# A fused four-layer kernel: in layer 0, x in one tile per half of the channels, convolutions in even steps, the result's projection in two parts, layer norms one chunk ahead

## The chip, the cores and the metric

The kernel runs on one core of a Trainium2 chip. The metric is the device time of one execution in microseconds (us), as the median over executions. The engines are named as in the profile: PE (TensorE), with its weight loads PEld, DVE (VectorE), ACT (ScalarE), POOL (GpSimd) and SP (SyncE), which here issues nearly all DMA transfers. Each engine works through its own queue in program order; semaphores order one engine against another.

## The reference, cut to what matters

Four layers follow each other on a tensor x of 2 x 128 x 64 x 64 (batch, channels, height, width), all in float32. The change touches layer 0 alone: a layer norm over the channels, four selective scans (Mamba) with the same weights over the 4096 positions of each image, row by row and column by column, each forward and reversed, and a fused projection that is added to x.

```python
xz = x @ W_in.T
xh, z = jnp.split(xz, 2, axis=-1)                 # 256 channels each
xc = causal_depthwise_conv(xh, conv_w) + conv_b   # 4 taps
xh = silu(xc)
x_dbl = xh @ W_xp.T                               # dt (8), B (16), C (16)
dt = softplus(dt @ W_dt.T + b_dt)
dA = exp(dt[..., None] * A)                       # 256 channels x 16 states
dBu = dt[..., None] * Bm[:, :, None, :] * xh[..., None]
h = dA_t * h + dBu_t                              # the scan over positions
y = einsum('lbdn,bln->bld', hs, Cm) + xh * Dp
y = y * silu(z)
return y @ W_out.T                                # then W_fuse, b_fuse, + x
```

Layer 1 and layer 2 are attention over 4096 positions, layer 3 is a small Mamba over channel groups with a group norm.

## The kernel before, in words

Layer 0 cuts the positions into chunks of T = 512. There are 2 images x 2 orders (by rows, by columns) x 2 directions x 8 = 64 chunks, one after the other; the list `chunks` (L432) has eight forward chunks, then eight reversed ones, and so on. The channels (256) lie in two halves `i` of 128 partitions. For the scan, channels and states are regrouped into 16 units `u` of 128 partitions x 1024 elements, and one unit is done in each of the 16 steps `s` of a chunk.

The order of all work is written out by hand (`manual_schedule`, L447). In step `s` of chunk `c` the loop emits, on each engine's queue:

- POOL: `s_dbu(s+2)` (L336), the product of `dus` and `bs` into one of three `dbu` buffers; `s_hc(s-1)` for the units 1, 5, 9, 11 and 14 (L390).
- DVE: `s_scan(s)` (L380), then what the table `V` holds for this step, then `s_hc(s-1)` for the other units (L392). After step 2 the old chunk's second half is gated with `yg_(1)`, after step 10 this chunk's first half with `yg_(0)` (L410).
- ACT: `s_da(s+1)` (two exponentials, L349), `s_fix(s+1)` (L361, L364), `s_hst(s-1)` (L385), then what the table `A` holds.
- PE: `s_pc` in odd steps (L369), `y0` (L396), `s_y` for pairs of units (L403; the pairs 4,5 in step 8 and 6,7 in step 9), then what the table `M` holds.
- SP: the spreads of dt and dt*x (`dts`, `dus`) and of the rows of B and C (`bs`, `cs`) for the next chunk.

The tables hold the work on three other chunks: the rest of the chunk before (`old`), the step sizes of the next chunk (`new`: `pt`, `abs_`, `dt_`, `dtu_`, and `pz`, `z_` for forward chunks), and the convolution of the chunk after it (`nxt`). The convolution is four matmuls per half with the taps folded into the weights, `px(i)` (L238); ACT moves the result with its bias into SBUF, `x_(i)` (L244); later come one `xsilu` over both halves (L257) and the projection `pd` (L273).

Each PSUM bank is in use: four for `da`, two for `pc`, one for `y`, one for `misc`. So all of `px`, `pz`, `pt`, `pd`, `po` and the layer norm's matmuls share one `misc` buffer, and each has to wait until the one before it has been read. The tile `xs` (both halves, 128 x 2 x 512) has two buffers, so `x_` of chunk k+2 writes where the `xs` of chunk k was, whose last readers are `y0(0)` in step 3 and `y0(1)` in step 11.

`y0` adds the skip term with a diagonal matrix, `s_y` sums the states into `y`, `yg_` multiplies with the gate, `po` (L412) projects both halves and adds x through the identity, all into `misc`, and `xo` (L426) writes x back. The layer norm of a chunk (`Norm0`: `center`, `sub`, `square`, `var`, `keep`, `ln`, `exp`, `rows`, `scale`, `mul`, `affine`) is spread over the end of one chunk and the beginning of the next; the first three are done ahead of the loop. Norms are in flight in chunks 0 to 5 and 15 to 23 (counted from 0).

```python
                if nxt is not None:
                    M[9], A[10] = lambda: nxt.px(0), (lambda: nxt.x_(0),)
                    M[11], A[12] = lambda: nxt.px(1), (lambda: nxt.x_(1),)
                    A[13] = (nxt.xsilu,)
                    M[15] = nxt.pd
```

Of the kernel before, what the change touches and what calls it, by code (L numbers as in the profile page):

```python
# [13 lines left out]
P = 128  # L14
B, C, H, W = 2, 128, 64, 64
L = H * W
T = 512
# [5 lines left out]
ND = 73  # L23
# [33 lines left out]
def conv_seq_kernel(ctx: ExitStack, tc: tile.TileContext, a: dict, out: bass.AP):  # L57
# [36 lines left out]
    with ExitStack() as c0:  # L94
# [9 lines left out]
        def wt(tag, bufs=None, shape=(P, 2, T)):  # L104
            return wk_.tile(list(shape), F32, tag=tag, name=tag, bufs=bufs)
# [110 lines left out]
        class Chunk:  # L216
# [4 lines left out]
            def __init__(self, b, order, rev, q):  # L221
                self.b, self.order, self.rev = b, order, rev
                self.first, self.last = q == 0, q == NCH - 1
                self.ci = NCH - 1 - q if rev else q
                self.t0 = self.ci * T
                self.src = xnt if order else xn

                self.beg, self.sec = (T - 1, 0) if rev else (0, 1)
                self.dbu, self.h, self.hc = {}, {}, {}
                self.bs, self.cs, self.dts, self.dus = {}, {}, {}, {}  # L230
                self.pt_, self.y, self.pc = {}, {}, {}


            def px(self, i):
# [4 lines left out]
                       start=(k == 0), stop=(k == 3))  # L239

            def x_(self, i):
                if i == 0:
                    self.xs = wt("xs")
                act(self.xs[:, i, :], self.px_, AF.Identity, bias=v(f"cb{i}"))  # L244

            def pz(self, i):
                self.pz_ = misc()
# [6 lines left out]
                nc.scalar.copy(self.sz[:, i, :], self.pz_)  # L254

            def xsilu(self):
                act(self.xs, self.xs, AF.Silu)  # L257

            def zsilu(self):

# [8 lines left out]
            def pd(self):  # L269

                self.p = misc()
                for i in range(2):
                    mm(self.p[:ND], lhsT=w_xpT[:, i, :], rhs=self.xs[:, i, :],  # L273
                       start=(i == 0), stop=(i == 1))

            def xd_(self):
# [39 lines left out]
            def dtu_(self, i):  # L316
                if i == 0:
                    self.dtu = wt("dtu", 1)
                    self.ddu = dr.tile([2, P, T], F32, tag="ddu", name="ddu")
                nc.gpsimd.tensor_mul(self.dtu[:, i, :], self.dt[:, i, :], self.xs[:, i, :])  # L320
                nc.sync.dma_start(self.ddu[i], self.dtu[:, i, :])

            def spread(self, what, i):
# [69 lines left out]

            def y0(self, i):
                self.y[i] = ps.tile([P, T], F32, tag="y", name="y")
                mm(self.y[i], lhsT=diag_d[:, i, :], rhs=self.xs[:, i, :], start=True,  # L396
                   stop=False, skip_group_check=True)

            def s_y(self, u):
# [9 lines left out]
                    self.yg = wt("dt", 1)  # L409
                nc.vector.tensor_mul(self.yg[:, i, :], self.sz[:, i, :], self.y[i])  # L410

            def po(self):  # L412
                d = 2 * self.order + self.rev
                p = self.pp = misc()
                for i in range(2):
                    mm(p, lhsT=wof[:, i, d, :], rhs=self.yg[:, i, :], start=(i == 0), stop=False)
                if self.order:
                    xo = x[:, self.b, :].rearrange("p (h w) -> p w h", w=W)
                    xo = xo[:, self.ci * 8 : self.ci * 8 + 8, :]
                    p = p.rearrange("p (w h) -> p w h", h=H)  # L420
                else:
                    xo = x[:, self.b, self.t0 : self.t0 + T]
                mm(p, lhsT=ident, rhs=xo, start=False, stop=True)
                self.xo_ = xo, p

            def xo(self):  # L426
                if self.order == 0 and not self.rev:
# [6 lines left out]
        nk = len(chunks)  # L434
        norms, gates = {}, {}
        for j in range(NCH):
            if j > 2:
                norms[j - 3] = Norm0(0, j)
            norms[15 + j] = Norm0(1, j)
        turns = {k: k % 8 for k in (*range(6, 14), *range(32, 40))}  # L440

# [3 lines left out]
            pairs.setdefault(max(m + (3 if m in POOL_HC else 2) for m in (u, u + 1)), []).append(u)  # L445

        with tc.manual_schedule():  # L447
            for j in range(3):
                n = Norm0(0, j)
                for f in (n.center, n.sub, n.square, n.var, n.keep, n.ln, n.exp, n.rows, n.scale,  # L450
                          n.mul, n.affine):
                    f()
            c, c1 = chunks[:2]
            for i in range(2):
                c.px(i)
# [27 lines left out]
            c.s_dbu(1)  # L483
            c.s_da(0)
            c.s_fix(0)
            for i in range(2):
                c1.px(i)
                c1.x_(i)
# [3 lines left out]
            for k, c in enumerate(chunks):  # L492
                new, nxt = (chunks[k + i] if k + i < nk else None for i in (1, 2))
                ln, lp = norms.get(k), norms.get(k - 1)

                def at(u):
                    return (c, u) if 0 <= u < 16 else ((old, u + 16) if u < 0 else (new, u - 16))

                A, V, M, G = {}, {}, {}, {}
                if old is not None:
                    M[3], A[4] = old.po, (old.xo,)
                if c.rev:
                    A[4] = (*A[4], c.zload)
                else:
                    A[8] = (c.zsilu,)
                if new is not None:
                    A[0] = (new.xd_,)
                    M[0], A[1] = lambda: new.pt(0), (lambda: new.abs_(0),)  # L510
                    M[1], A[2] = lambda: new.pt(1), (lambda: new.abs_(1), new.e_exp)
                    A[3] = (new.e_ln,)
                    M[4], V[5] = lambda: new.pt(0), lambda: new.dt_(0)
                    M[5], V[6] = lambda: new.pt(1), lambda: new.dt_(1)
                    G[7], G[8] = lambda: new.dtu_(0), lambda: new.dtu_(1)
                    if not new.rev:
                        M[6], A[7] = lambda: new.pz(0), (lambda: new.z_(0),)
                        M[13], A[14] = lambda: new.pz(1), (lambda: new.z_(1),)
                if nxt is not None:
                    M[9], A[10] = lambda: nxt.px(0), (lambda: nxt.x_(0),)  # L520
                    M[11], A[12] = lambda: nxt.px(1), (lambda: nxt.x_(1),)
                    A[13] = (nxt.xsilu,)
                    M[15] = nxt.pd
                if lp is not None:
                    A[3] = (*A[3], lp.ln, lp.exp)
                    A[6] = (lp.rows,)
                    M[7], V[8] = lp.scale, lp.mul
                    A[9] = (lp.affine,)
                if ln is not None:
                    M[12], V[13] = ln.center, ln.sub  # L530
                    A[14] = (*A.get(14, ()), ln.square)
                    M[14], A[15] = ln.var, (ln.keep,)
                if k in turns:
                    A[11] = (lambda: turn(turns[k]),)

                for s in range(16):
                    (c1, u1), (c2, u2), (cp, up) = at(s + 1), at(s + 2), at(s - 1)

                    if c2 is not None:
                        c2.s_dbu(u2)  # L540
                    c.s_scan(s)
                    if s in V:
                        V[s]()
                    if cp is not None:
                        cp.s_hc(up)
                    if s in G:
                        G[s]()

                    if c1 is not None:
                        c1.s_da(u1)  # L550
                        c1.s_fix(u1)
                    if cp is not None:
                        cp.s_hst(up)
                    for f in A.get(s, ()):
                        f()

                    if s % 2 and s < 15:
                        c.s_pc(s + 1)
                    elif s == 15 and new is not None:
                        new.s_pc(0)  # L560
                    if s in (3, 11):
                        c.y0(s // 11)
                    for cy, e in ((c, s), (old, s + 16)):
                        for u in pairs.get(e, ()) if cy is not None else ():
                            cy.s_y(u)
                            cy.s_y(u + 1)
                    if s in M:
                        M[s]()

                    if s == 2 and old is not None:  # L570
                        old.yg_(1)
                    if s == 10:
                        c.yg_(0)

                    if new is not None:
                        if s in (7, 14):
                            new.spread("dts", s // 14)
                        if s in (9, 13):
                            new.spread("dus", s // 13)
                        if s in (8, 10, 12, 14):  # L580
                            new.states(0, s // 2 - 4)
                        if s in (11, 12, 13, 15):
                            new.states(1, GROUPS_C[{11: 0, 12: 1, 13: 2, 15: 3}[s]])
                old = c
            c.s_hc(15)
            for e in (16, 17):
                for u in pairs.get(e, ()):
                    c.s_y(u)
                    c.s_y(u + 1)
            c.yg_(1)  # L590
            c.po()
            c.xo()

# [890 lines left out]
```

## Time and profile before

| what | value |
|---|---|
| time, median of 3 runs | 7136.85 us (7136.01 to 7143.56) |
| the profiled execution's own time | 7116.64 us |
| its span | 7114.9 us |
| PE busy over the span | 6064.8 us (85%) |
| DVE busy | 5525.5 us (78%) |
| POOL busy | 5366.2 us (75%) |
| ACT busy | 4446.3 us (62%) |
| layer 0's scans, first start to last | about 106 to 3795 us |

The span runs from the first to the last instruction; the execution's own time is 1.7 us more, and the median of the unprofiled runs is 20.2 us above the profiled execution. Busy shares are means over stages with different limits, so the stage of the change, layer 0, is read by itself and chunk by chunk. In the timeline a row is a group of equal instructions: its start, its length, engine, line, output and inputs, count, and in brackets the idle time of the engine ahead of it with what ended that. A float32 matmul is two records on PE, so a convolution half (four matmuls) is a row of x8.

### The profile page before, as it was taken

Reading aid. Unit: us, or ns where it says so; the run is one execution under the profiler, and the core shown is the slowest. Engines: PE = TensorE matmul, PEld = TensorE weight load, DVE = VectorE, ACT = ScalarE, POOL = GpSimd, SP = SyncE. Lnnn points to the kernel's source line nnn. Section 1 sums busy time; section 2 is a strip of 40 time slices with the busy share of each in tenths; the row PEclk is TensorE's granted clock in tenths of the full one; section 3 lists DMA queues with packets and bytes.
Section 4 is the critical chain, followed back from the end, with each engine's and each line's share of the span. In section 5 each row is a group of like instructions: output and inputs, shape, how many; then the busy total and the mean of one; then the engine's idle time right before and its main releaser. Section 6 shows DMA issues by size and latency. Waiting matters only on the chain. (4 is left out here: it accounts for less than half of the span.)

```text
span 7114.9 us, 67194 instructions
## 1 busy us (share of the span) xinstructions
PE 6064.8 (85%) x20656; PEld 2821.4 (40%) x20656; DVE 5525.5 (78%) x4494; ACT 4446.3 (62%) x7622; POOL 5366.2 (75%) x2487
## 2 busy tenths in 40 slices
PE   6877778887788877888777999999999998889898
PEld 2222222222222222222223887788778886222222
DVE  3889888888898898989895666566556665778787
ACT  4777777777777777787675565455456555443443
POOL 3889888888998889989995666555556665777676
PEclk7777777777777777777777999999999999898898
DMA  4555555555555555555552000000000000222222
GB/s 121 133 134 139 134 131 134 134 137 134 137 142 141 141 139 144 138 134 140 144 143 76 1 5 2 1 1 1 1 1 1 13 1 30 79 75 70 91 67 77
DMA packets 352651, 616.50 MB, mean 87 GB/s; under 512 B 72473, under 2 KB 74786, under 8 KB 351906
## 3 DMA queue, kind: packets, MB, share of 16 engines
q1 hardware_dynamic: 351552, 610.44, 32.8%
q8 instruction: 162, 2.65, 0.2%
q14 instruction: 199, 1.63, 0.1%
q10 hardware_dynamic: 738, 1.78, 0.1%
HBM read 496.45 MB, written 115.47 MB: 86 GB/s over the span
## 5 line engine op out<-in xcount | busy, mean ns | idle before, releaser
L336 POOL TENSOR_TENSOR dbu<-dus,bs 128x1024 f32<-128x1024 f32 x1024 | 2402.2, 2359 | 422.2 <-DVE h L380 357.7
L380 DVE TENSOR_TENSOR_SCAN h<-da,hst,dbu 128x1024 f32<-128x1024 f32 x896 | 2093.1, 2342 | 355.2 <-ACT dbu L364 218.4
L349 ACT ACTIVATE da<-dts,aneg 128x512 f32<-128x512 f32 (+1 forms) x2048 | 1409.3, 688 | 304.1 <-DVE h L380 266.0
L826 POOL TENSOR_TENSOR sum<-sum,sc 128x1024 f32<-128x1024 f32 x384 | 905.8, 2359 | 495.9 <-ACT sc L821 492.2
L788 ACT COPY sc<-s 128x512 f32<-128x512 f32 x1024 | 597.0, 584 | 867.6 <-PE s L783 755.0
L369 PE MATMUL pc<-xd,sel 16*128 16x512 f32 x1024 | 760.8, 831 | 360.4 <-DVE hc L392 357.8
L783 PE MATMUL s<-q,k 128*128 128x256 f32 x4096 | 1057.5, 382 | 11.7 <-ACT q L769 8.4
L838 PE MATMUL av<-sc,v 128*128 128x256 f32 x4096 | 1049.6, 379 | 2.2 <-ACT sc L821 2.2
L795 DVE TENSOR_TENSOR mx<-mx,s 128x512 f32<-128x512 f32 x896 | 609.2, 680 | 569.1 <-ACT sc L788 568.1
L392 DVE TENSOR_TENSOR hc<-h,pc 128x1024 f32<-128x1024 f32 x704 | 841.5, 1195 | 0.1
L783 PEld LDWEIGHTS s<-q,k 128*128 128x128 f32 x4096 | 780.7, 191 | 146.1 <-issue 36.6
L838 PEld LDWEIGHTS av<-sc,v 128*128 128x128 f32 x4096 | 769.1, 190 | 103.1 <-ACT sc L821 3.7
L403 PE MATMUL y<-hc,cst 128*32 128x512 f32 x4096 | 766.3, 785 | 5.3 <-POOL hc L390 3.1
L390 POOL TENSOR_TENSOR hc<-h,cs 128x1024 f32<-128x1024 f32 x320 | 754.9, 2359 | 1.3 <-issue 1.3
L1153 POOL TENSOR_TENSOR A<-A,D 128x1024 f32<-128x1024 f32 x224 | 525.6, 2363 | 224.9 <-DVE D L1158 200.2
L818 DVE TENSOR_TENSOR sc<-sc,pm 128x1024 f32<-128x1024 f32 x512 | 620.1, 1212 | 0.9 <-PE pm L814 0.9
L821 ACT ACTIVATE sc<-sc 128x1024 f32<-128x1024 f32 x512 | 542.0, 1059 | 8.6 <-DVE sc L818 8.1
L1146 ACT ACTIVATE A<-dtr,aneg 128x1024 f32<-128x1024 f32 (+1 forms) x256 | 245.8, 1031 | 379.1 <-PE y L1178 361.6
L369 PEld LDWEIGHTS pc<-xd,sel 16*128 16x128 f32 x1024 | 186.6, 226 | 704.9 <-issue 291.3
L293 PE MATMUL misc<-xd,w_dt 9*128 9x512 f32 x512 | 335.5, 739 | 131.8 <-ACT xd L278 49.5
L1130 PE MATMUL q<-xs,lb 32*128 32x512 f32 x896 | 330.5, 710 | 70.4 <-DVE D L1140 64.2
L1164 DVE TENSOR_TENSOR A<-A,q 128x1024 f32<-128x1024 f32 (+1 forms) x256 | 276.6, 1080 | 138.5 <-PE q L1130 138.3
(210 smaller groups left out, 8070.2 us busy)
## 6 DMA issues: line engine op xcount, KB each, us to landing
dts<-ddt SPq DMA_DIRECT2D x512, 256.0 KB, 4.8
dus<-ddu SPq DMA_DIRECT2D x512, 256.0 KB, 4.8
bs<-rows SPq DMA_DIRECT2D x1024, 64.0 KB, 4.8
cs<-rows SPq DMA_DIRECT2D x1024, 64.0 KB, 3.1
ddt<-dt SPq DMA_DIRECT2D x128, 256.0 KB, 2.0
ddu<-dtu SPq DMA_DIRECT2D x128, 256.0 KB, 2.3
dtr<-ddt SPq DMA_DIRECT2D x448, 64.0 KB, 1.9
rx<-ddx SPq DMA_DIRECT2D x448, 64.0 KB, 1.9
```

The source lines that it names most:

```text
L336: nc.gpsimd.tensor_mul(t, self.dus[q], _bc(self.bs[g], 1, [P, 2, T]))
L349: act(t[:, i, sl], self.dts[q][:, i, sl], AF.Exp, scale=an[:, g, 2 * q + i : 2 * q + i + 1])
L369: mm(t, lhsT=sel[32:48, 4 * g : 4 * g + 4, :].rearrange("p n d -> p (n d)"), rhs=self.xd[32:48, :], start=True, stop=True)
L380: nc.vector.tensor_tensor_scan(ho, ai, bi, init, ALU.mult, ALU.add)
L390: nc.gpsimd.tensor_mul(t, self.h[u], _bc(self.cs[gq(u)[0]], 1, [P, 2, T]))
L392: nc.vector.tensor_mul(t, self.h[u], _bc(self.pc[u // 2], 1, [P, 2, T]))
L403: mm(self.y[q // 2][r : r + 32, :], lhsT=sum4, rhs=self.hc[u][:, i, :], start=False, stop=(u % 8 >= 6), skip_group_check=True)
L783: mm(p[:, o, :], lhsT=j.k[m // 8][:, m % 8 * P : m % 8 * P + P], rhs=self.q, start=True, stop=True)
L795: nc.vector.tensor_max(self.mx, self.s[0][:, 0:2, :] if u == 1 else self.mx, self.p[u])
L818: nc.vector.tensor_sub(s, s, _bc(self.pm[:, :], 1, [P, 4, NQ]))
L826: nc.gpsimd.tensor_add(self.sum, self.s[0] if w == 1 else self.sum, self.s[w])
L838: mm(self.av, lhsT=self.job.v[m // 8][:, m % 8, :], rhs=self.s[u // 2][:, m % 4, :], start=(m == 0), stop=(m == 31))
```

## The change

- `xs` becomes two tiles, one per half, each with two buffers. `xsilu` becomes two instructions.
- `px(0)`, `px(1)` go from steps 9 and 11 to steps 8 and 10; `x_(0)` from step 10 to step 9, `x_(1)` stays in step 12. `affine` goes from step 9 to step 10.
- `po` is cut in two: `po_x` (x through the identity, now first) in step 2, the two projections in step 3. `y0(0)` goes from step 3 to step 4.
- Layer norms of the first image run one chunk earlier: the norm of chunk 3 is done ahead of the loop, after the first `s_da` and `s_fix`, and norms are in flight in chunks 0 to 4. Those of the second image stay.

```diff
@@ Chunk
             def x_(self, i):
-                if i == 0:
-                    self.xs = wt("xs")
-                act(self.xs[:, i, :], self.px_, AF.Identity, bias=v(f"cb{i}"))
+                self.xs[i] = wt(f"xs{i}", shape=(P, T))
+                act(self.xs[i], self.px_, AF.Identity, bias=v(f"cb{i}"))
...
             def xsilu(self):
-                act(self.xs, self.xs, AF.Silu)
+                for t in self.xs.values():
+                    act(t, t, AF.Silu)
...
-            def po(self):
-                d = 2 * self.order + self.rev
-                p = self.pp = misc()
-                for i in range(2):
-                    mm(p, lhsT=wof[:, i, d, :], rhs=self.yg[:, i, :], start=(i == 0), stop=False)
+            def po_x(self):
+                self.pp = p = misc()
...
-                mm(p, lhsT=ident, rhs=xo, start=False, stop=True)
+                mm(p, lhsT=ident, rhs=xo, start=True, stop=False, skip_group_check=True)
                 self.xo_ = xo, p
+
+            def po(self):
+                for i in range(2):
+                    mm(self.pp, lhsT=wof[:, i, 2 * self.order + self.rev, :], rhs=self.yg[:, i, :],
+                       start=False, stop=(i == 1), skip_group_check=True)
@@ norms
-            if j > 2:
-                norms[j - 3] = Norm0(0, j)
+            if j > 3:
+                norms[j - 4] = Norm0(0, j)
@@ ahead of the loop
             c.s_da(0)
             c.s_fix(0)
+            norm(3)
             for i in range(2):
                 c1.px(i)
                 c1.x_(i)
@@ in the loop
                 if old is not None:
-                    M[3], A[4] = old.po, (old.xo,)
+                    M[2], M[3], A[4] = old.po_x, old.po, (old.xo,)
...
                 if nxt is not None:
-                    M[9], A[10] = lambda: nxt.px(0), (lambda: nxt.x_(0),)
-                    M[11], A[12] = lambda: nxt.px(1), (lambda: nxt.x_(1),)
+                    M[8], A[9] = lambda: nxt.px(0), (lambda: nxt.x_(0),)
+                    M[10], A[12] = lambda: nxt.px(1), (lambda: nxt.x_(1),)
                     A[13] = (nxt.xsilu,)
                     M[15] = nxt.pd
                 if lp is not None:
                     A[3] = (*A[3], lp.ln, lp.exp)
                     A[6] = (lp.rows,)
                     M[7], V[8] = lp.scale, lp.mul
-                    A[9] = (lp.affine,)
+                    A[10] = (lp.affine,)
...
-                    if s in (3, 11):
+                    if s in (4, 11):
                         c.y0(s // 11)
```

The readers `pd`, `dtu_` and `y0` take `self.xs[i]` for `self.xs[:, i, :]`, and the last chunk calls `po_x` ahead of `po`.

## The prediction

> **What bounds the kernel now.** First I read the windows view over single chunks of layer 0: chunk 36 (forward, no norm), chunk 59 (reversed, no norm) and chunk 19 (with a norm).
>
> ```profile
> core 0: us, PE busy (x) PEld busy (x) DVE busy (x) ACT busy (x) POOL busy (x), PEclk, DMA share, GB/s
> 2214.90:2272.90 58.00, 47.29 (x123) 13.19 (x122) 51.26 (x32) 46.10 (x89) 51.26 (x24) 0.74 0.54 138
> 3521.70:3579.40 57.70, 45.26 (x125) 11.85 (x118) 51.04 (x33) 40.78 (x81) 51.27 (x24) 0.71 0.56 138
> 1226.30:1287.70 61.40, 50.82 (x135) 14.64 (x136) 52.50 (x34) 47.99 (x98) 51.49 (x24) 0.75 0.52 130
> ```
>
> A chunk takes 57 to 61 us, and no engine is busy for more than 52.5. DVE and POOL are the nearest bounds at 51; the other 6 us are stalls. So next the waits of DVE, ACT and POOL over layer 0 (us in total, times, longest).
>
> ```profile
> DVE h L380 <- ACT dbu L364: 218.4, 193, 4.6
> DVE h L380 <- ACT hst L385: 148.6, 38, 4.8
> ACT xs L244 <- PE y L396: 413.9, 62, 7.9
> POOL dbu L336 <- DVE h L380: 357.7, 310, 3.0
> ```
>
> The scan on DVE waits for ACT, and ACT's longest wait is `x_` for `y0`, 62 times: once in each chunk that has a `nxt`. POOL only waits for the scan. The timeline of chunk 59, steps 9 to 12, shows how the one becomes the other.
>
> ```profile
> 3553.29 2.04 PE L369 MATMUL pc<-xd,sel 16*128 16x512 f32 x2 [4.71 <-DVE hc L392]
> 3555.26 1.94 PE L403 MATMUL y<-hc,cst 128*32 128x512 f32 x8
> 3557.12 5.55 PE L238 MATMUL misc<-xnt,wk 128*128 128x512 f32 x8
> 3558.69 0.66 DVE L410 TENSOR_TENSOR dt<-sz,y 128x512 f32<-128x512 f32 x1
> 3562.60 1.12 PE L369 MATMUL pc<-xd,sel 16*128 16x512 f32 x2
> 3563.65 1.12 PE L396 MATMUL y<-xs,diag_d 128*128 128x512 f32 x2
> 3564.82 0.69 ACT L244 ACTIVATE xs<-misc,vec 128x512 f32<-128x512 f32 x1 [7.57 <-PE y L396]
> 3565.40 1.41 ACT L349 ACTIVATE da<-dts,aneg 128x511 f32<-128x511 f32 x2
> 3567.22 4.59 DVE L380 TENSOR_TENSOR_SCAN h<-da,hst,dbu 128x1024 f32<-128x1024 f32 x2 [4.49 <-ACT hst L385]
> ```
>
> `x_(0)` is ready for its data at 3562.7, when `px(0)` ends, but writes into the `xs` buffer that `y0(1)` still has to read, and PE does that one step later. `da(12)` stands behind it on ACT, so scan 12 starts 4.49 us late. Reading this idle ahead of scan 12 in every chunk gives 242 us in 62 chunks: 4.02 on average in the 30 reversed chunks without a norm, 3.92 in the 19 forward ones without, 3.61 in the 13 with one. The other idle ahead of scans is 63 us at step 5 (the tables for `e_ln`), 42 at step 15 (the tables for `xsilu`) and 32 at step 2 (`pd`), which the change leaves alone.
>
> **The change, part by part.**
>
> *xs in two tiles.* `y0(0)` reads its half in step 4 and `x_(0)` writes in step 9; `x_(1)` stays in step 12, behind `y0(1)` of step 11. The wait of 6 to 8 us on ACT goes. The bytes are the same. One more ACT instruction per chunk: 1.06 us becomes two of 0.59 to 0.69 (the 512-wide rows of lines 300, 175 and 244), +0.12 to +0.32 us on the path at step 15, 7 to 20 us in 62 chunks. Against it, `da(14)` followed `x_(1)` 0.31 us after scan 12 had ended (3569.88 against 3569.57) and need not any more. I take zero, and -12 to +19 for the range.
>
> *px one step earlier.* Now `x_(0)` waits for `px(0)` instead, with `da(11)`, `s_fix(11)` and so scan 11 behind it on ACT; and on PE `pc(10)` and the `s_y` of units 6 and 7 stand behind `px(0)`, with `yg_(0)` on DVE waiting for them. So I walk the queues. `px(0)` starts when `s_y` of units 4 and 5 ends (the `misc` buffer is free by then): 3548.58 in chunk 59, 2245.10 in chunk 36, 1261.81 in chunk 19. It takes 5.0 us (the mean of the rows 5.55, 5.54, 4.35 in these chunks and 4.72 in chunk 15), `pc(10)` and `s_y` 2.1 more (1.12 and 1.06 at full clock). So `y` is ready at 3555.7, 2252.2, 1268.9; `yg_(0)` ran at 3558.69, 2251.65, 1267.34. Late by nothing (3.0 us of cover), 0.6 and 1.6 us. `x_(0)` ends 0.7 after `px(0)`, `da(11)` and its fix take 1.8: 2252.6 in chunk 36 against scan 11 at 2252.23 before, inside the 0.6. `x_(1)`: `px(1)` (3.70) follows `s_y`, then `pc(12)` and `y0(1)` (1.12 each), all done about 6 us after `yg_(0)`; scan 14, the first behind it, comes about 8.5 later (scans 11 to 13, two `hc`). Free. If the cover is gone, each us that PE is late at step 9 costs a us in that chunk.
>
> *What is late next.* With scan 12 moved up by 4, POOL must hold: after scan 5 it ran without a gap to 3567.54 in chunk 59, then waited 2.11 and 0.94 us for DVE. Without the stall it goes on, and `dbu` 13, 14, 15 end at about 3562.9, 3565.2 and 3569.9, each before its scan (3565, 3568, 3572). DVE stays the bound. `dus` for the next chunk lands at 3563.6 and is first read at 3572.0: 8.4 us of slack, of which 2 to 4 go.
>
> *po in two, y0(0) later.* The matmuls are the same. `po_x` waits for `abs_(1)` to free `misc` (3531.3), about when PE took up `y0` before (3531.5); `pc(4)` behind it has until step 5. `xo` waited for PE only 15 us in total over the kernel. Zero; with the cover gone at most the 1.9 us of the identity matmuls per chunk, which would come back at the wait of ACT's tables at step 5.
>
> *Norms ahead.* Chunk 5 loses its norm: it took 59.6, those after it 56.9, so -2.5. Ahead of the loop, PE takes norm 3 before `px` of chunk 1. `square` can start when `da(0)` ends at 100.58; from `square` to the end of `mul` the first norm took 10.05 (22.33 to 32.38), so `px` starts at 110.6, not 95.88. ACT's `da(1)` and scan 1 stand behind: +14.8 us once (10 if it overlaps better).
>
> No moved step issues a DMA, so SP's queue keeps its order.
>
> **Sum.** 242 removed, less 19 x 0.6 = 11 and 13 x 1.6 = 21, plus 2.5, less 14.8: 198 us. Against the profiled execution's own 7116.64 that is 6919; the unprofiled median stands 20.2 above it, so I forecast 7136.85 - 198 = 6939. Its own range, with the two costs of `px` between zero and double and the bounds above, is 6895 to 6995.
>
> **Clock, row and rule.** PE's clock decides how long `px(0)` takes. In chunk 36 the windows view shows:
>
> ```profile
> 2239.90:2243.30 3.40, 3.40 (x8) 0.63 (x10) 3.40 (x3) 2.76 (x8) 3.40 (x3) 0.50 0.20 77
> 2246.70:2250.20 3.50, 3.50 (x11) 0.58 (x10) 3.34 (x3) 3.42 (x7) 3.50 (x2) 0.50 1.06 270
> 2250.20:2253.60 3.40, 3.40 (x5) 1.34 (x5) 3.40 (x3) 0.94 (x3) 3.40 (x3) 0.50 1.05 321
> 2253.60:2257.00 3.40, 3.40 (x9) 1.05 (x7) 2.08 (x2) 0.00 (x0) 3.40 (x2) 1.00 1.07 237
> ```
>
> PE is busy throughout a stretch (the number behind the comma), yet the granted clock (third from last) is half until `px(0)` has filled a stretch. The Trainium skill ("TensorE: Matmul & The Clock Gate", Part 1) says that one busy window of some 3.4 us lifts the gate; here `pc` and `s_y` on part of the array did not lift it, and where they differ I go by the rows.
>
> **Rivals.**
> - *A warm convolution.* PE has no pause ahead of `px(0)` any more and runs it at full clock, 3.70 as `px(1)` does. Late by 0, 0 and 0.3 us: 242 - 4 + 2.5 - 14.8 = 226, 6911. By the skill's rule the time would come out here. For it: chunk 19 turned fast while `s_y` and `px(0)` shared a stretch. Against it: the rows above. 0.18.
> - *Half the stall stays.* Of ACT's 7.57 us, only the 2.15 behind `px(0)` (3562.67 to 3564.82) are `y0` and `pc`; if ACT gets to `x_(0)` ahead of a late `px(0)` as it does now, 2 us per chunk are won: 124 + 2.5 - 14.8 = 112, 7025. Against it: PE stood idle 4.71 us before `pc(10)` in chunk 59. This is also the case in which the split tile does not do what it says. 0.12.
> - *A cold convolution.* `px(0)` at half clock is twice the row of four records (3.62 for `po`), 7.0 with the overlap taken off, then 2.07 and 1.94: `y` is late by 0.7, 4.2 and 5.3 us. 242 - 21 - 80 - 69 + 2.5 - 14.8 = 60, 7077. 0.09.
> - *Slower.* The cold case, and PE reaches step 8 late as well, since 47 us of PE work at this clock then fill 53 us instead of 58. Each us late costs 62; from 1 us on the kernel is slower, and at 2 us it is 60 - 124 = -64: 7201. Against it: what PE waits for ahead of step 8 (`dt_`, the `hc` of unit 5) is set by DVE and POOL. 0.05.
>
> **Numbers.** The forecast has 0.56. The range 6880 to 7045 takes in the warm and the half case and leaves 0.14 and some edges out. Differences of up to 0.2% (14 us) count as no change, about what a measurement of this kernel can tell. All cases but the last are faster by more; between the cold and the slower case lie a few in a hundred: faster 0.92, same 0.03, slower 0.05.
>
> **What would show it.** Right: line 244 no longer waits for line 396, no idle ahead of scan 12, at most 2 us ahead of scan 11 in norm chunks, reversed chunks of 53 us, scan 1 at about 127 instead of 112. Wrong: `yg_` or scan 11 waiting for PE by 2 us or more in most chunks, POOL waited for by the scan, or chunks still at 57.

## The result

| | before | changed |
|---|---|---|
| median of the runs shown together | 7139.19 us (7136.01 to 7143.56) | 6914.52 us (6907.13 to 6921.35) |
| ratio, 95% interval | | 0.9685 (0.9668 to 0.9701) |
| span of the profiled execution | 7114.9 us | 6919.6 us |
| layer 0, up to the end of the last write of x | 3803.45 us | 3592.20 us |
| the rest (layers 1 to 3, same code) | 3311.4 us | 3327.4 us |

The kernel is 225 us faster; 198 were forecast. In the profiles layer 0 alone lost 211 us, and the other layers, whose code is the same, took 16 us longer. Over all 14 profiles of this study those layers took between 3311 and 3333 us, so a profiled span is compared best up to the end of layer 0. Below, "layer 0's end" is that point; two executions of the changed kernel put it at 3592.20 and 3595.45.

The windows view of the changed kernel, over one chunk each: the forward chunk 36, the reversed chunk 59 and the norm chunk 19.

```profile
core 0: us, PE busy (x) PEld busy (x) DVE busy (x) ACT busy (x) POOL busy (x), PEclk, DMA share, GB/s
2093.60:2147.90 54.30, 46.29 (x126) 12.41 (x122) 51.18 (x32) 46.31 (x90) 51.22 (x24) 0.78 0.58 147
3324.50:3378.50 54.00, 45.59 (x125) 11.68 (x118) 51.11 (x33) 41.09 (x82) 51.73 (x24) 0.75 0.59 149
1163.30:1221.30 58.00, 49.44 (x135) 14.22 (x134) 52.58 (x34) 48.30 (x98) 51.44 (x24) 0.79 0.54 136
```

The busy time of DVE and POOL is what it was (51 to 52.6 us); the chunks are 3.4 to 3.7 us shorter. So it is idle time that went. The mean periods over layer 0 say the same: 30 reversed chunks 56.88 to 52.87, 19 forward ones 57.05 to 54.48, and 13 counted here as chunks with a norm (0 to 5 and 16 to 22) 61.24 to 58.08. Two of these 13 differ from the rest: chunk 0 takes in the longer start (59.97 to 66.88), and chunk 5 loses its norm (59.57 to 53.64).

The waits of the changed kernel over layer 0 (us in total, times, longest) name what is left.

```profile
POOL dbu L336 <- DVE h L380: 192.6, 191, 14.9
DVE h L380 <- ACT dbu L364: 120.1, 158, 2.9
ACT xs L243 <- PE misc L238: 71.0, 36, 5.8
DVE dt L312 <- PE pc L369: 19.5, 34, 1.2
DVE dt L410 <- issue: 16.0, 16, 1.7
DVE dt L410 <- PE y L403: 12.0, 12, 1.2
```

The scan's 148.6 us behind ACT's `hst` (line 385) and `x_`'s 413.9 behind `y0` are gone, but for 43.5 us of the latter, all of it ahead of `x_(1)` (in chunk 36 at 2137.26, 0.86 us behind `y0(1)`). POOL still only waits for the scan, 193 us instead of 358. Two waits of DVE are new: the gate `yg_(0)` (L410) and the step size `dt_` (L312). The first was in the forecast; the second wasn't. For the gate the view names PE's sums only in part and puts more to "issue", that is, to nothing that the profile shows; that PE's order is behind nearly all of it follows from the run with the sums first, below.

The timeline of the changed kernel, chunk 59, steps 8 to 12, against the rows of before in the prediction:

```profile
3351.62 4.47 PE L238 MATMUL misc<-xnt,wk 128*128 128x512 f32 x8
3357.64 0.68 ACT L243 ACTIVATE xs<-misc,vec 128x512 f32<-128x512 f32 x1
3359.16 3.70 PE L238 MATMUL misc<-xnt,wk 128*128 128x512 f32 x8
3359.30 1.42 ACT L349 ACTIVATE da<-dts,aneg 128x511 f32<-128x511 f32 x2 [0.98 <-DVE h L380]
3366.50 4.59 DVE L380 TENSOR_TENSOR_SCAN h<-da,hst,dbu 128x1024 f32<-128x1024 f32 x2
```

`px(0)` fills what was idle time of PE, `x_(0)` writes at 3357.64 without waiting, `da` follows, and the scans of steps 12 and 13 (the row x2) run one behind the other with no bracket, where scan 12 had 4.49 us before.

### The profile page after: what moved, and what is told of

It reads as the page before. It is cut to its first block, busy times and chain, and to the rows that moved or that the text cites. A ratio compares the mean times of both kernels' runs of the same rounds, so it can differ in the third digit from the quotient of the medians.

```text
span 6919.6 us, 67264 instructions
## 1 busy us (share of the span) xinstructions
PE 6036.7 (87%) x20656; PEld 2806.4 (41%) x20656; DVE 5525.2 (80%) x4494; ACT 4467.5 (65%) x7688; POOL 5366.3 (78%) x2487
## 5 line engine op out<-in xcount | busy, mean ns | idle before, releaser
L369 PE MATMUL pc<-xd,sel 16*128 16x512 f32 x1024 | 723.1, 792 | 241.4 <-DVE hc L392 241.1
L403 PE MATMUL y<-hc,cst 128*32 128x512 f32 x4096 | 725.2, 711 | 60.5 <-POOL hc L390 57.7
L369 PEld LDWEIGHTS pc<-xd,sel 16*128 16x128 f32 x1024 | 180.7, 219 | 622.1 <-DVE hc L392 271.6
L293 PE MATMUL misc<-xd,w_dt 9*128 9x512 f32 x512 | 304.2, 675 | 63.0 <-ACT xd L278 50.7
```

The source lines that it names most:

```text
L369: mm(t, lhsT=sel[32:48, 4 * g : 4 * g + 4, :].rearrange("p n d -> p (n d)"), rhs=self.xd[32:48, :], start=True, stop=True)
L403: mm(self.y[q // 2][r : r + 32, :], lhsT=sum4, rhs=self.hc[u][:, i, :], start=False, stop=(u % 8 >= 6), skip_group_check=True)
```

## The experiments

Theory A said that the stall had two causes in a row: `x_(0)` waits for `px(0)`, and had that been early, for `y0(1)` in the joint tile. Theory B gave all of it to one of them. "Scan-12 idle" is DVE's idle time ahead of scan 12, summed over 62 chunks; it was 242.0 us before and is 0 in the changed kernel.

### The changed kernel once more

The edit: none; a second measurement of the changed kernel, on the chip of the next three.

> The changed kernel itself, beside the next three on one chip. Both theories: 0.969 of the kernel before, 6905 to 6920 us; its second profile tells whether layer 0 alone (211 us less in the first pair of profiles) carries the gain, and how much the later layers vary by themselves.

Measured: 6915.67 us, 0.9703 (0.9689 to 0.9718) of before (7129.83). Layer 0's end 3595.45. What follows is compared with 6915 and 3592 to 3595.

### The split tile alone

On the kernel before:

```diff
-                if i == 0:
-                    self.xs = wt("xs")
-                act(self.xs[:, i, :], self.px_, AF.Identity, bias=v(f"cb{i}"))
+                self.xs[i] = wt(f"xs{i}", shape=(P, T))
+                act(self.xs[i], self.px_, AF.Identity, bias=v(f"cb{i}"))
...
```

> The kernel before with x in one tile per half and nothing else: px stays in steps 9 and 11, x_(0) in step 10. Theory A (the stall had two parts in a row: x_(0) waits for px(0), and then for y0(1), which stands behind px(0) on PE): only the part behind px(0) goes, 2.1 us of the 4.0 ahead of scan 12 in 62 chunks, 130 us: about 7005, and some 2 us stay ahead of scan 12, now for line 238. Theory B (the shared buffer alone was the stall): all 242 us go, 6895 to 6905, faster than the whole change.

Measured: 7022.97 us, 0.9850 (0.9836 to 0.9863); layer 0's end 3693.95, 109.5 earlier than before. Scan-12 idle fell from 242 to 102. The timeline of this kernel in a forward chunk:

```profile
3401.88 4.97 PE L238 MATMUL misc<-xnt,wk 128*128 128x512 f32 x8
3406.89 0.69 ACT L243 ACTIVATE xs<-misc,vec 128x512 f32<-128x512 f32 x1 [4.89 <-PE misc L238]
3409.29 4.59 DVE L380 TENSOR_TENSOR_SCAN h<-da,hst,dbu 128x1024 f32<-128x1024 f32 x2 [1.81 <-ACT hst L385]
```

`x_(0)` no longer waits for `y0(1)`, but has to wait 4.89 us for `px(0)` itself, and the scan is still 1.81 us late. Theory A's size (7005) was nearly met. What it had left out, and it missed by 18 us, is step 15: the idle ahead of scan 15 rose from 42 to 95 us. Behind the rows above, `x_(1)` waits 1.45 us for `px(1)`, which stays in step 11, then `xsilu` and its tables follow on ACT, and scan 15 is late by 1.96 us.

### The earlier convolution alone

On the kernel before, with the joint tile; `px(1)` stays in step 11, and the norms go ahead as in the change:

```diff
-                    M[9], A[10] = lambda: nxt.px(0), (lambda: nxt.x_(0),)
+                    M[8], A[10] = lambda: nxt.px(0), (lambda: nxt.x_(0),)
...
```

> The kernel before with px(0) in step 8 and the norms one chunk ahead, but x still in one tile for both halves, x_(0) in step 10 and px(1) in step 11. Theory A: y0(1) no longer stands behind px(0) and runs about 2.2 us after yg_(0) has ended, so scan 12 is late by some 1.4 us instead of 4.0: 160 us less, 33 more ahead of yg_(0), 12 more ahead of the loop: about 7020. Theory B: x_(0) waits for y0(1) as before, the gap stays: 7150 to 7185.

Measured: 6995.13 us, 0.9813 (0.9797 to 0.9828); layer 0's end 3671.18, 132.3 earlier. From its waits:

```profile
ACT xs L244 <- PE y L396: 242.4, 62, 5.2
```

Still 62 waits for `y0`, now 242 us instead of 414: ACT waits for the right thing from an earlier time, because PE comes to `y0(1)` without the late convolution ahead of it. Scan-12 idle is 43.7, step 15's 81.1. Theory B (slower than before) fell; A's 7020 was 25 us too slow. Either half alone brings 107 to 135 us, and both 214, or 247 once the loss shown below is mended. Neither alone ends the idle ahead of scan 12, and together they do: this is shown, and with it that the stall had both causes. That the two gains sum to 242 is in part chance, for they don't simply add: scan-12 idle alone fell by 140 and by 198 us, more together than the 242 there were (the earlier `px(0)` brings `y0(1)` forward too), and each kernel has 39 to 53 us more idle ahead of scan 15.

### y0(0) back in step 3

On the changed kernel. Why is `dt_` late? One suspect was `y0(0)`, which now stands in the same step as `pt(0)` on PE, ahead of it.

```diff
-                    if s in (4, 11):
+                    if s in (3, 11):
```

> The changed kernel with y0(0) back in step 3, ahead of po on PE; po stays in two parts. Theory A (y0(0) and the first sums moved behind po make pt(0), and so dt_ in step 5, late; 34 waits of line 312 for PE, 19.5 us in the changed kernel): these go, 10 to 20 us less than the changed kernel, 6895 to 6905. Theory C (that wait only shows what scan 5 would lose to ACT's tables anyway): within 5 us of the changed kernel, with more idle ahead of scan 5 or 6 in its place.

Measured: 6919.67 us, 0.9708 (0.9694 to 0.9721); layer 0's end 3595.85. No different from the changed kernel; theory A's gain of 10 to 20 us didn't come. The wait of `dt_` is still there, 27.6 us instead of 19.5, so the place of `y0(0)` isn't its cause.

### The sums ahead of pc in step 9

On the changed kernel, for the new wait of `yg_(0)`: in step 9 the `s_y` of units 6 and 7 go ahead of `pc(10)`.

```diff
-                    if s % 2 and s < 15:
+                    if s % 2 and s < 15 and s != 9:
...
+                    if s == 9:
+                        c.s_pc(10)
```

> The changed kernel with, in step 9 on PE, the sums of units 6 and 7 ahead of pc(10), not behind it; px(0) stays ahead of both. Theory A (the new wait of yg_(0), 33 us over layer 0, is for sums that stand behind px(0) and pc(10)): pc(10) takes 1.1 to 2.0 us, so of the waits of up to 1.7 us nearly all go: 20 to 30 us less than the changed kernel, 6885 to 6895. Theory D (the time is lost to px(0) itself, or scan 11 would wait for ACT anyway, since da(11) stands behind x_(0)): within 8 us of the changed kernel, with idle ahead of scan 11 in its place.

Measured: 6901.79 us, 0.9686 (0.9669 to 0.9703) of its own before (7128.66); layer 0's end 3581.98, 10 to 13 earlier. The idle ahead of `yg_(0)` went from 33.4 us to 1.3, but 14.5 us came back ahead of scan 11, in forward and norm chunks. So this wait does cost time, some 10 to 14 of the 33 us that it shows, which lies between the two theories. By the medians alone the two intervals (this kernel's and the changed one's, each against its own before) overlap; layer 0's end and the last two runs below point the same way.

### pt(0) ahead of the sums in step 4

On the changed kernel, to bring `dt_(0)` forward on PE:

```diff
+                    if s == 4 and s in M:
+                        M.pop(s)()
                     for cy, e in ((c, s), (old, s + 16)):
```

> The changed kernel with pt(0) ahead of the sums of units 0 and 1 in step 4 on PE. The step before (y0(0) ahead of po) only made xo wait for PE and dt_ stayed late. Theory A (pt(0) is late by the 1.07 us of these sums): it starts when xo has freed the buffer, 0.8 us earlier, and the 19 us of idle ahead of dt_ in step 5 go: 6895 to 6905. Theory C (xo sets it): less than 6 us, dt_ late as before.

Measured: 6936.37 us, 0.9728 (0.9707 to 0.9748); layer 0's end 3622.40, some 28 later. Both theories missed: neither had it slower. The wait of `dt_(0)` went, and a larger one came one step behind it, for `dt_(1)` in step 6 (this kernel's waits):

```profile
DVE dt L312 <- PE misc L293: 44.3, 26, 2.4
```

Two things differ on PE. `pt(0)` now waits for `xo` (0.82 us in chunk 59) with the sums behind it, where the sums had filled that time; and `pt(0)` and `pc(6)`, which had stood next to each other and ran at the same time, are parted. The run doesn't say how much is due to which.

### The norms not ahead

On the changed kernel, the layer norms in the chunks of before, `affine` in step 8:

```diff
-            if j > 3:
-                norms[j - 4] = Norm0(0, j)
+            if j > 2:
+                norms[j - 3] = Norm0(0, j)
...
-            norm(3)
...
-                    A[10] = (lp.affine,)
+                    A[8] = (lp.affine, *A.get(8, ()))
```

> The changed kernel with the norms of the first image not ahead: three ahead of the loop, and affine in step 8 (ahead of zsilu on ACT) so that px(0) of step 8 can read it. Theory A (norm 3 ahead of the loop costs 12 to 13 us, and in-loop it costs less): 12 us back ahead of the loop, some 2 us in each of chunks 1 to 5 and 3 in chunk 5 lost, for affine holds zsilu and da(10) on ACT: within 5 us of the changed kernel. Theory E (in-loop norms are hidden): 10 to 13 us less than it.

Measured: 6918.2 us, 0.9703 (0.9687 to 0.9719); layer 0's end 3601.77. The start is quicker again (4.1 us ahead of scan 1 of chunk 0 instead of 15.0), and 21 us come up ahead of scan 10 in the norm chunks. Theory A held (within 5 us). By the medians the norms' move is worth nothing either way; by layer 0's end it may be worth 6 to 10 us.

### The projection whole again

On the changed kernel, `po` in one piece in step 3 and `y0(0)` in step 3, as before; the split tile and the early convolutions stay.

```diff
-                    M[2], M[3], A[4] = old.po_x, old.po, (old.xo,)
+                    M[3], A[4] = old.po, (old.xo,)
...
-                    if s in (4, 11):
+                    if s in (3, 11):
```

> The changed kernel with po in one part again in step 3, x last, and y0(0) in step 3. Theory A (the split of po moves the same matmuls and hides nothing): within 8 us of the changed kernel; the wait of dt_ in step 5 stays at 10 to 25 us. Theory F (the early x part is what keeps xo and the tables on time): 20 to 60 us more, as idle ahead of scan 5 or of dt_.

Measured: 6889.39 us, 0.9666 (0.9651 to 0.9682); layer 0's end 3570.34, 22 to 25 earlier than the changed kernel. Both expectations missed: cutting `po` in two the way the change does it isn't free and doesn't help; it costs some 25 us. The idle ahead of `dt_` is gone with it (1.2 us).

What differs on PE shows in the timeline of the kernel before, chunk 59, with `pt(1)` (L293) of step 1 and `pc(4)` (L369) of step 3:

```profile
3529.15 0.69 PE L293 MATMUL misc<-xd,w_dt 9*128 9x512 f32 x1
3529.16 0.69 PE L369 MATMUL pc<-xd,sel 16*128 16x512 f32 x1
3529.69 0.59 PE L293 MATMUL misc<-xd,w_dt 9*128 9x512 f32 x1
3529.69 0.59 PE L369 MATMUL pc<-xd,sel 16*128 16x512 f32 x1
```

and in the changed kernel, the same place of chunk 59:

```profile
3332.18 1.57 PE L293 MATMUL misc<-xd,w_dt 9*128 9x512 f32 x2
3334.44 2.07 PE L420 MATMUL misc<-x,cst 128*128 128x512 f32 x2 [0.69 <-ACT e L300]
3336.45 2.07 PE L369 MATMUL pc<-xd,sel 16*128 16x512 f32 x2
3338.45 3.78 PE L425 MATMUL misc<-dt,wof 128*128 128x512 f32 x4
3345.60 0.69 DVE L312 SCALAR_TENSOR_TENSOR dt<-misc,e 128x512 f32<-128x512 f32 x1 [0.65 <-PE pc L369]
```

Before, the two matmuls stand next to each other and their records start within 0.01 us: both are done in 1.13 us, from 3529.15 to 3530.28. `pt` reads 9 partitions from 64 on and `pc` 16 from 32 on. The change puts `po_x` (L420) between them, and `pc(4)` takes 2.07 us by itself, with `po` behind it, and behind that `pt(0)`, on which `dt_` waits 0.65 us. The Trainium skill ("TensorE: Matmul & The Clock Gate", Part 3, on the mechanism) says that matmuls in different row groups of the array run at the same time; the rows agree, 1.13 us for two against 1.12 for one `pc` alone at full clock.

This became theory G: it isn't the cut of `po` that costs, but the lost neighbour. The next two runs separate `pc(4)` from the cut. But `pc(4)` loses more than its neighbour. Before, PE stood idle behind the pair, for 1.26 us in this chunk (until `yg_(1)` had freed `y`), so `pc(4)` ran in time that PE had to spare, at a granted clock of 0.95. In the changed kernel PE waits ahead of `po_x` (0.69 us), and `pc(4)` comes behind that wait, at a granted clock of 0.50, with everything up to `pt(0)` queued behind it.

### The pair restored, the projection still in two

On the changed kernel, `pc(4)` goes to step 2, ahead of `po_x` and so next to `pt(1)`:

```diff
+                    if s == 2:
+                        c.s_pc(4)
-                    if s % 2 and s < 15:
+                    if s % 2 and s < 15 and s != 3:
```

> The changed kernel with pc(4) emitted in step 2 ahead of po_x, next to pt(1) of step 1; po stays split, y0(0) in step 4. Theory G (the split costs because po_x stands between pt(1) and pc(4): side by side the two small matmuls run at once, 1.1 to 1.8 us for both; alone pc(4) takes 2.07, and pt(0) and dt_ are late by it): the 19 us of idle ahead of dt_ in step 5 go as in the kernel with po whole, 6888 to 6900. Theory H (the order of the two parts of po or y0(0) behind them costs): dt_ stays late, 6908 to 6922.

Measured: 6882.14 us, 0.9659 (0.9644 to 0.9675); layer 0's end 3566.95, 25 to 28 earlier than the changed kernel, with `po` still in two. Its timeline in a reversed chunk:

```profile
3307.61 0.75 PE L293 MATMUL misc<-xd,w_dt 9*128 9x512 f32 x1
3307.62 0.76 PE L369 MATMUL pc<-xd,sel 16*128 16x512 f32 x1
3309.90 2.08 PE L420 MATMUL misc<-x,cst 128*128 128x512 f32 x2 [0.68 <-ACT e L300]
3319.09 0.69 PE L293 MATMUL misc<-xd,w_dt 9*128 9x512 f32 x1 [2.00 <-ACT x L432]
3320.33 0.67 DVE L312 SCALAR_TENSOR_TENSOR dt<-misc,e 128x512 f32<-128x512 f32 x1
```

The records start side by side again, PE gets to `pt(0)` with 2.00 us to spare, and `dt_` doesn't wait. Theory H, that the order of `po`'s parts or `y0(0)` behind them costs, is out; the time is 6 us below G's range.

Whether it is the neighbour or the place, another kernel of this study tells. In the kernel with the split tile alone, where `po` is whole and `pc(4)` stands ahead of the wait, `pc(4)` often starts so late that it hardly runs beside `pt(1)`. Its timeline, chunk 59:

```profile
3428.49 1.12 PE L293 MATMUL misc<-xd,w_dt 9*128 9x512 f32 x2
3429.46 1.12 PE L369 MATMUL pc<-xd,sel 16*128 16x512 f32 x2
3432.30 2.07 PE L396 MATMUL y<-xs,diag_d 128*128 128x512 f32 x2 [1.72 <-DVE dt L410]
```

In 24 of the chunks 1 to 61 the two share 0.3 us or less there, and in each PE still stands idle for 0.78 to 1.72 us behind `pc(4)`; the idle ahead of `dt_` is 3.3 us in the whole kernel. So the overlap can go and cost next to nothing, as long as `pc(4)` stays ahead of PE's wait. So the gain of this run comes more from the place in the queue than from the neighbour.

### The pair parted, the projection whole

The control: on the kernel with `po` whole, `pc(4)` goes behind `y0(0)` in step 3, away from `pt(1)`.

```diff
-                    if s % 2 and s < 15:
+                    if s % 2 and s < 15 and s != 3:
...
+                    if s == 3:
+                        c.s_pc(4)
```

> The changed kernel with po whole and y0(0) in step 3 (the faster version, 6889), and pc(4) moved behind y0(0), away from pt(1). Theory G: the idle ahead of dt_ comes back without any split, 15 to 25 us: 6904 to 6915. Theory H: 6885 to 6893.

Measured: 6972.92 us, 0.9783 (0.9766 to 0.9800); layer 0's end 3648.78, 78 later than with the pair. The direction is G's, the size is far above its 15 to 25. The edit again does both things: it parts the pair and puts `pc(4)` behind PE's wait for `yg_(1)`. The waits of this kernel show two places:

```profile
ACT x L430 <- PE misc L423: 82.0, 48, 10.2
DVE dt L312 <- PE pc L369: 77.2, 58, 2.7
```

With the pair, the same two came to 11.2 us (2 times) and 1.2. Here `po` is late too, so `xo` waits for it, and `pt(0)` can have the `misc` buffer only after `xo`: PE's idle time, which had been cover, became a chain through PE, ACT and PE again. PE's own wait for `xo` ahead of `pt(0)` (lines 293 and 430) is a gauge of that cover: 62.9 us with the pair, 4.8 without (and 3.0 in the changed kernel against 101.9 in the one with the pair restored, there lines 293 and 432).

### Both repairs, the projection whole

The kernel with `po` whole, and the sums of step 9 ahead of `pc(10)`:

```diff
-                    if s % 2 and s < 15:
+                    if s % 2 and s < 15 and s != 9:
...
+                    if s == 9:
+                        c.s_pc(10)
```

> Two edits that helped alone, together: po whole with y0(0) in step 3, and in step 9 the sums of units 6 and 7 ahead of pc(10). They act in different steps, so their gains should add: 26 and 14 us less than the changed kernel, about 6875; idle ahead of yg_(0) near zero.

Measured: 6882.93 us, 0.9653 (0.9636 to 0.9669); layer 0's end 3551.41, 19 earlier than without the second edit. The median is 8 us above the 6875 expected and 6 below that kernel's; the idle ahead of `yg_(0)` is 1 us.

### Both repairs, the projection in two

The changed kernel with the pair restored and the sums first:

```diff
+                    if s == 2:
+                        c.s_pc(4)
-                    if s % 2 and s < 15:
+                    if s % 2 and s < 15 and s not in (3, 9):
...
+                    if s == 9:
+                        c.s_pc(10)
```

> As the run before, but with po split and pc(4) next to pt(1). Theory G: the split itself costs nothing then, within 8 us of the run before. Theory H: 15 us or more slower than it.

Measured: 6867.4 us, 0.9637 (0.9621 to 0.9654); layer 0's end 3554.37. This is the fastest kernel of the study, 48 us below the changed one and 262 below the one before on its chip. The two repairs add up: 33.5 and 13.9 us alone, 48.3 together. Against the whole projection its median is 15 us lower, but its layer 0 ends 3 us later, so whether `po` in one piece or in two is better, once the pair stands, stays open (G's band of 8 us was missed, on the fast side). From 500 to 3400 us DVE and POOL are each busy for 96% of the time (2779 and 2785 of 2900 us; 89% before), so little is left to take out by order alone.

## Why the prediction was right, and where it was wrong

DVE's idle time, summed chunk by chunk over layer 0, stands against the terms of the sum:

| term | forecast, us | measured, us |
|---|---|---|
| idle ahead of scan 12 | -242 | 242.0 to 0 |
| `yg_(0)` late | +32 (forward 11, norm 21, reversed 0) | 0 to 33.4 (16.3, 13.2, 3.9) |
| prologue | +14.8 | +13.3 |
| xs in two tiles, step 15 | 0 | 42.1 to 32.3 |
| **po in two, y0(0) later** | **0** | **`dt_` idle 1.1 to 19.2; 22 to 28 of layer 0's end** |
| tables in step 5, `pd` in step 2 | left alone | 62.6 to 57.4, 31.6 to 22.7 |

**The stall.** Right in mechanism and size: of `x_`'s 413.9 us behind `y0` 43.5 are left, scan 12 has no idle time, and the two half experiments show that both the tile and the step had to change. Half of the change came out near the price of the rival "half the stall stays" (112 there, 107 and 135 measured), though with other parts in it: more of scan 12's idle went, and step 15 took some back.

**The new wait at `yg_(0)`.** Right in total, wrong in its parts: forward chunks were dearer, norm chunks cheaper. The run with the sums first shows that this wait is real time, though more than half of it only takes the place of waits behind it, ahead of scan 11 above all.

**The prologue.** 1.5 us less than worked out. Scan 1 came at 125.25 (forecast about 127). Chunk 5, which lost its norm, took 53.6 us, like the other forward chunks (54.48).

**The step that failed: "po in two, y0(0) later. The matmuls are the same."** The matmuls are the same; their order on PE isn't. The step asked when `po_x` could start and whether `pc(4)` was due by step 5, that is, whether `pc(4)` was in time for its own reader. It did not ask what stands behind `pc(4)` then: `po`, `xo`, `pt(0)` and `dt_`. The bound of 1.9 us per chunk was put on the identity matmuls; the dear part was `pc(4)`, 2.07 us at half the clock on that chain, where before it had run in time that PE had to spare. And it hit `dt_` through `pt(0)`, not the tables. Moving `pc(4)` alone, with `po` still cut, brings the time back, and moving it alone, with `po` whole, loses it: this is shown. That the lost overlap with `pt(1)` is what costs is not: both runs change the place and the neighbour at once, and the chunks without overlap in the split-tile kernel speak for the place.

**The clock.** `px(0)` was put at 5.0 us for all. Its mean went from 5.09 to 4.15 in reversed chunks, from 5.16 to 5.24 in forward ones and from 4.96 to 4.65 in those with a norm. So the rival "a warm convolution" (3.70 everywhere) holds for 20 of the 30 reversed chunks and 2 of the others, the ones with the full clock granted throughout; its time, 6911, is close to what was measured, but not for its reason, since `yg_(0)` still cost 33 us and not 4. The Trainium skill's rule ("TensorE: Matmul & The Clock Gate", Part 1) that a busy window of about 3.4 us lifts the gate would make `px(0)` warm in forward chunks too, but for its start; their 5.24 us speak against it here. In chunk 36 PE was busy for all of 2120.98 to 2124.40, and the granted clock was 0.50 until 2127.81. The prediction also took 3.70 us for `px(1)`, which held before; in the changed kernel it took a mean of 4.38 in reversed chunks and 4.17 in forward ones, so part of what `px(0)` gained in clock `px(1)` lost.

**The sum.** The rows above, with 3.7 us that went ahead of scan 13, come to -206.6 us from scan 0 of chunk 0 to scan 0 of chunk 62 (11.5 of the prologue's 13.3 lie in that stretch); it became 210.1 us shorter (3586.4 to 3376.3). What the missing 3.5 us are stays open. That the forecast of 198 lies near layer 0's 211 is partly luck: steps 2, 5 and 15 lost 24 us of idle time that the forecast had left alone, and `dt_` took 18 that it had put at nothing. With `pc(4)` ahead of `po_x` the gain was 247, by the medians. That the medians differ by 225 and layer 0 by 211 lies where no profile of one execution can show it: the profiled execution of before was 23 us below its median, that of the changed kernel 7 above.

## What to carry to other kernels

When a wait is taken away, ask what the waiting instruction would have waited for next: here a buffer and a late producer stood in a row, and each repair alone brought about half. Before an instruction that has to wait is put into a queue, look what moves behind that wait: `pc(4)` cost nothing while it ran in idle time ahead of the wait, and its whole length behind it. And compare stages whose code is unchanged across runs first, to know how much of a difference in span belongs to nobody.

## What the runs showed of the hardware

- Two float32 matmuls of different steps, over 9 and 16 partitions of the same tile, can run at the same time when they stand next to each other on PE's queue: 1.13 us for both (kernel before, chunk 59), against 1.12 for one at full clock and 2.07 at half clock. In the kernel before their records start together in 38 of the chunks 1 to 61.
- PE could be busy without a gap for 3.42 us, most of it with matmuls on 16 rows or 32 columns of the array, and the granted clock stayed at 0.50 for the 3.41 us after that (changed kernel, 2120.98 to 2127.81).
- One activation over 1024 elements per partition takes 1.06 us; two over 512, one behind the other, took 1.15. Cutting it in two cost 0.09 us, less than the 0.12 to 0.32 worked out from single rows.
- Layers 1 to 3, with the same code, took 3311 to 3333 us in 14 profiles.
